# A four-layer graph network in fp32 on one core: whole-array transposes, a tanh kept in PSUM, one copy of s2 and an eleventh tile buffer

## The chip, the cores and the metric

The kernel runs on one core of a Trainium2 chip. The metric is the device time of that core in microseconds (us), as the median of several runs. All data are fp32.

## The reference

The input `x` has 64 graphs of 256 nodes with 128 features, and one weighted adjacency matrix `adj` (256 x 256) serves them all. Four layers follow each other; each takes `h = relu(layernorm(x))` and adds its result to `x`.

```
layer 0:  s1, s2 = h W1^T, h W2^T          (W from adj, 256 outputs e)
          e_ij = sum_e a_e leaky(s1_ie + s2_je + b_e) + adj_ij      (slope 0.2)
          x += sigmoid(softmax_j(e) h)
layer 1:  x_h = elu(h Wi + bi)
          e_ij = sigmoid(tgt_i + src_j + be) * mask_ij
          recv = elu([e x_h, x_h * sum_j e] Wn + bn);  x += [recv, x_h] Wm + bm
layer 2:  A = adj * exp(8 tanh((h q)(h k)^T / sqrt(128) / 8)), rows divided by their sums
          x += A h v
layer 3:  five steps of a gated unit: m = adj h; z, r = sigmoids, candidate = tanh; then x += h
```

The bulk of the work is `leaky(s1_ie + s2_je + b_e)` for all pairs of nodes: 64 graphs x 256 x 256 pairs x 256 values of e.

## The kernel before

**Layer 0's pairs.** A tile is one node i against all 256 nodes j of its graph, with 128 of the 256 values of e on the partitions: 128 x 256 elements. Eight tiles (four groups g, two halves ic) make a batch, which lies in one buffer `r` of the pool `rp` with `BUFS` = 10 buffers. Tiles are made by three engines: ACT with a Relu and a bias (line 620), POOL with a min and a max (line 625), DVE four tiles at a time from a copy `s2_dve` of `s2` in PSUM (line 608, half a batch). PE then multiplies a batch by `a_win` (line 673, `multiply`), four matmuls of N = 512, one for each group of 32 PSUM partitions, into the bank `e_ps`. Each fp32 matmul stands in the profile as two records of 128*32 (128 rows, 32 columns of the array), so a batch has eight records. A graph has 32 rows t and two values of ec for each, 64 batches. Where five complete batches (`SPARE`) wait for PE, `begin` makes the next row a merged one: the tiles of ec = 0 are made, and DVE adds those of ec = 1 into the same buffer (`merge`, line 642, eight instructions), so that PE has one batch to multiply in place of two. A merge thus moves work from PE to DVE.

**The rest of the layers** runs beside this, as Python generators that yield the engine which comes next: `head` and `senders` prepare layer 0's operands for the coming graphs, `softmax0` ends layer 0 of a graph, `layer1`, `layer2` and `layer3` follow for a group of two graphs (four blocks of 128 nodes; the first two and last two groups are of one graph). Each `Chain` runs its generators one after another at a pace in ns for each step: 2200 for layers 1 and 2 (`chain12`), 2400 for layer 3, 2500 for `softmax0`.

**The order of instructions** on all engines is fixed when the program is built. A planner (`Model`, and the loop at the end of the kernel) keeps a time for each engine, adds a cost in ns for every instruction, and always emits what can start first. `dve`, `act`, `pool`, `mm` hold these costs, `LAG` is the time from one engine to the next, and `MARGIN` gives paced steps of PE another 300. At run time each engine takes its instructions in that order and waits on semaphores.

**Matmuls and transposes.** `mm` splits every matmul into four, one for each group of 32 columns of the array:

```
        model.op("pe", max(n, 64) * 1.676)
        for c in range(4):
            nc.tensor.matmul(
                out[bass.ts(c, 32), :], lhsT=lhsT[:, bass.ts(c, 32)], rhs=rhs, **flags
            )
```

`tr` transposes a 128 x 128 block as such a matmul with the identity `ident` on the moving side. It serves `transpose_blocks` (tiles h0t, h_t, h3t), `softmax0` (`pm` into `e_ps`, which it reuses as `pt_ps`) and `layer3` (`hn_ps` after each of four steps, `y_ps` at the end).

**Layer 1's scores.** `tgt_ps`, one matmul for the group, lies in the single bank of `ps_a`; ACT writes `th = tanh(...)` for each graph to SBUF (line 793), and DVE makes `e_t` of it and of the mask `mask_h` (line 801). All of layers 1 and 2 take their PSUM from that one bank.

Of the kernel before, what the change touches and what calls it, by code (L numbers as in the profile page):

```python
# [16 lines left out]
FLT_MAX = 3.4028234663852886e38  # L17
STEPS = 5
INV_SQRT_D = 1.0 / (128.0 ** 0.5)
BUFS = 10  # L20
SPARE = 5
MARGIN = {"pe": 300}
MEMORY = 7000
# [30 lines left out]
def kernel(ctx: ExitStack, tc: tile.TileContext, ins: dict, out: bass.AP):  # L54
# [21 lines left out]
    def psum_a(shape, name):  # L76
        return ps_a.tile(shape, F32, tag="ps_a", name=name)
# [30 lines left out]
            )  # L108

    def tr(out, src):  # L110
        mm(out, lhsT=src, rhs=ident, start=True, stop=True)


    firsts = [sum(GROUPS[:g]) for g in range(len(GROUPS))]
# [328 lines left out]
    def transpose_blocks(space, src, tag, banks):  # L443

        yield "pe"
        G, _, W = sizes(src)
        tp = banks([P, G, P], tag + "_ps")
        for g in range(G):
            tr(tp[:, g, :], src[:, g, :])
        yield "act"  # L450
        t = space.tile([P, G, P], F32, tag=tag, name=tag)
        act(W).copy(t, tp)
        return t
# [77 lines left out]
    class Pairs:  # L531
# [36 lines left out]
        def own(self, who):  # L568

            if who == "dve" and who not in self.owned:  # L570
                t = self.owned[who] = ps_d.tile([P, 2, N], F32, tag="s2_dve", name="s2_dve")
                for ec in range(2):
                    dve(N).tensor_copy(t[:, ec, :], self.snd["s2"][:, ec, :])
            if who == "act":

                self.by_act += 1
                if self.by_act == 2:
                    t = self.owned[who] = ps_c.tile([P, 2, N], F32, tag="s2_act", name="s2_act")
                    act(2 * N, sbuf=1).copy(t, self.snd["s2"])
                if self.by_act <= 2:  # L580
                    return self.snd["s2"]
            return self.owned[who]
# [96 lines left out]
    def softmax0(g, b, of, e_ps, snd):  # L679


        h, xt = of["h"], xts[g]
        for ic in range(2):
            yield "dve", lambda: "adj_l" in snd

            if ic == 0:
                nmax = sp.tile([P, 2], F32, tag="nmax", name="nmax")
            dve(N, more=10).tensor_tensor_reduce(  # L688
                e_ps[:, ic, :], e_ps[:, ic, :], snd["adj_l"][:, ic, :], -1.0, FLT_MAX,
                ALU.add, ALU.min, nmax[:, ic : ic + 1],  # L690
            )
        for ic in range(2):
            yield "act"
            if ic == 0:
                pm = ap.tile([P, 2, N], F32, tag="pm", name="pm")
                rs = sp.tile([P, 2], F32, tag="rs", name="rs")
            act(N, 1, more=114).activation(  # L697
                pm[:, ic, :], e_ps[:, ic, :], AF.Exp, bias=nmax[:, ic : ic + 1], scale=-1.0,
                accum_out=rs[:, ic : ic + 1],
            )  # L700
        yield "dve"
        rh = sp.tile([P, 2], F32, tag="rh", name="rh")
        dve(2).reciprocal(rh, rs)
        yield "pe"
        pt_ps = e_ps
        for jc in range(2):
            for ic in range(2):
                tr(
                    pt_ps[:, jc, bass.ts(ic, P)], pm[:, ic, bass.ts(jc, P)]
                )  # L710
        yield "act"
        pt = ap.tile([P, 2, N], F32, tag="pt", name="pt")
        act(2 * N).activation(pt, pt_ps, AF.Copy, scale=0.5)
        yield "pe"
        o_ps = e_ps[:, :, 0:P]
        for ic in range(2):
            for jc in range(2):
                mm(
                    o_ps[:, ic, :], lhsT=pt[:, jc, bass.ts(ic, P)], rhs=h[:, b * 2 + jc, :],
                    start=(jc == 0), stop=(jc == 1),  # L720
                )
        for ic in range(2):
            yield "act"


            act(P, 2).activation(o_ps[:, ic, :], o_ps[:, ic, :], AF.Tanh, scale=rh[:, ic : ic + 1])
        yield "dve", lambda: counts["x1"] >= g - 2
        if b == 0:
            x1s[g] = ap.tile([P, 2 * GROUPS[g], P], F32, tag="x1", name="x1", bufs=3)
        x1 = x1s[g]  # L730
        dve(N).scalar_tensor_tensor(
            x1[:, bass.ts(b, 2), :], o_ps, 0.5, xt[:, bass.ts(b, 2), :], ALU.mult, ALU.add
        )
        if b == GROUPS[g] - 1:
            chain12.add(first_rest(g, x1))
# [16 lines left out]
    def layer1(x1):  # L752
# [8 lines left out]
        for b in range(NB):  # L761
# [13 lines left out]
            dve(2, 1).tensor_scalar(  # L775
                a_src[:, bass.ts(b, 2)], y_ps[:, :, P], 0.5, be_h, ALU.mult, ALU.add
            )
        yield "pe"
        tgt_ps = psum_a([P, W], "tgt_ps")
        mm(tgt_ps, lhsT=wt_rep, rhs=xh_t, start=True, stop=True)  # L780
        yield "pool"
        x1b = bp.tile([P, G, P], F32, tag="x1b", name="x1b")
        counts["x1"] += 1
# [1 line left out]
            x1b, x1, bm_bc.unsqueeze(1).to_broadcast([P, G, P]), ALU.add  # L785
        )

        ths, e_ts = [], []
        for b in range(NB):
            yield "act"  # L790
            th = bp.tile([P, 2, N], F32, tag="th", name="th", bufs=2)
            for jc in range(2):
                act(N, 1).activation(
                    th[:, jc, :], tgt_ps[:, bass.ts(b, N)], AF.Tanh,
                    bias=a_src[:, 2 * b + jc : 2 * b + jc + 1], scale=0.5,
                )
            ths.append(th)
        for b in range(NB):
            yield "dve"
            e_t = bp.tile([P, 2, N], F32, tag="e_t", name="e_t", bufs=2)  # L800
            dve(2 * N, more=200).scalar_tensor_tensor(e_t, ths[b], 1.0, mask_h, ALU.add, ALU.mult)
            e_ts.append(e_t)
        yield "pe"
        rsum_ps = psum_a([P, W], "rsum_ps")
# [106 lines left out]
    def layer3(x3, hn, h_t, home):  # L911
        G, NB, W = sizes(x3)
        hf = flat(h_t)
        for step in range(STEPS):
            yield "pe"
            m_ps = home.bank([P, W], "m_ps", step)
            for b in range(NB):
                for mc in range(2):
                    mm(
                        m_ps[:, bass.ts(b, N)], lhsT=hn[:, b * 2 + mc, :], rhs=adj_t[:, mc, :],  # L920
                        start=(mc == 0), stop=(mc == 1),
                    )
            g_ps = home.bank([P, W], "gate_ps", step + 1)
            mm(g_ps, lhsT=u3_t, rhs=hf, start=True, stop=False)
            yield "act"
            m_t = home.tile(W, "m_t", "m_t")
            act(W).copy(m_t, m_ps)  # L927
            yield "pe"
            mm(g_ps, lhsT=ws["w4_w"], rhs=m_t, start=False, stop=True)
            yield "act"  # L930

            t_r = m_ps
            act(W, 1).activation(t_r, g_ps, AF.Tanh, bias=br, scale=0.5)  # L933
            yield "dve"
            rh2 = home.tile(W, "rh2", "rh2")
            dve(W).scalar_tensor_tensor(rh2, t_r, 1.0, hf, ALU.add, ALU.mult)
            yield "pe"
            mm(
                g_ps, lhsT=w34_t, rhs=m_t, start=False, stop=True, skip_group_check=True
            )  # L940
            hv_ps = home.bank([P, W], "hv3_ps", step)
            mm(hv_ps, lhsT=ws["w5_w"], rhs=m_t, start=True, stop=False)
            mm(hv_ps, lhsT=u5_th, rhs=rh2, start=False, stop=True)
            yield "act"
            t_z, cand = g_ps, hv_ps
            act(W, 1).activation(t_z, g_ps, AF.Tanh, bias=bz, scale=0.5)  # L946
            yield "act"
            act(W, 1).activation(cand, hv_ps, AF.Tanh, bias=bh)  # L948

            yield "dve"  # L950
            df = home.tile(W, "rh2", "df")
            dve(W).tensor_tensor(df, cand, hf, ALU.subtract)
            yield "dve"
            zd = t_z
            dve(W).scalar_tensor_tensor(zd, t_z, 1.0, df, ALU.add, ALU.mult)
            yield "dve"
            hf_new = home.tile(W, "hf", "hf", 2)
            dve(W).scalar_tensor_tensor(hf_new, zd, 0.5, hf, ALU.mult, ALU.add)  # L958
            hf = hf_new
            counts["h3"] += step == 0  # L960
            if step < STEPS - 1:
                yield "pe"
                tp = home.bank([P, W], "hn_ps", step)
                for g in range(G):
                    tr(tp[:, bass.ts(g, P)], hf[:, bass.ts(g, P)])
                yield "act"
                hn = home.tile(W, "hn", "hn")
                act(W).copy(hn, tp)  # L968
                hn = hn.rearrange("p (g n) -> p g n", g=G)
        yield "pe"  # L970
        tp = home.bank([P, W], "y_ps", step)
        for g in range(G):
            tr(tp[:, bass.ts(g, P)], hf[:, bass.ts(g, P)])
        yield "dve"
        y = home.tile(W, "hn", "y").rearrange("p (g n) -> p g n", g=G)
        dve(W).tensor_tensor(y, tp.rearrange("p (g n) -> p g n", g=G), x3, ALU.add)
        return y
# [195 lines left out]
```

## Time and profile before

| What | Value |
|---|---|
| median of 3 runs | 5151.03 us (5151.01 to 5160.24) |
| the profiled execution | 5146.78 us |
| its span in the trace | 5144.3 us |
| granted TensorE clock | 0.998 |
| busy: PE, DVE, ACT, POOL | 98%, 97%, 98%, 95% |
| matmul records | 66800, of them 27632 of line 673 |
| DMA | 29.32 MB, mean 6 GB/s |

The profile is of one execution. "Busy" is the time in which at least one record of the engine is open. Records of PE, ACT and DVE overlap, because an instruction's record opens while the one before it still runs; so a mean duration is not the time that an instruction takes away from its engine, which is read from start to start in the timeline. A row of the costliest groups gives line, engine, operation, output and inputs, shapes and count, then busy us and mean ns of one, then the engine's idle time before them and what ended it. The windows give busy us and counts of PE, PE's weight loads, DVE, ACT and POOL in turn, then the granted clock, DMA's share and GB/s.

### The profile page before, as it was taken

The page shows a single profiled execution, that of the slowest core. Times are in us where ns is not written, and L with a number is a line of the kernel's source. Part 1 is how long each engine was busy: PE and PEld are TensorE (multiplying, and loading weights), DVE is VectorE, ACT ScalarE, POOL GpSimd, SP SyncE. Part 2 cuts the span into 40 slices and gives each one's busy share as a digit, 9 for nine tenths or more (in the row PEclk, how much of TensorE's full clock was granted, in tenths as well). Part 3 has the DMA queues.
Part 4 walks back from the last instruction along what each step waited for, and adds up shares of the span by engine and source line. Part 5 has one row for each costly group of instructions (what it writes and reads, how often), then busy time and mean ns, then how long its engine had stood idle before and what let it go on. Part 6 is the DMA issues. An engine that isn't in the chain of part 4 may idle for free. (4 is left out here: it accounts for less than half of the span.)

```text
span 5144.3 us, 172484 instructions
## 1 busy us (share of the span) xinstructions
PE 5063.0 (98%) x66800; PEld 2358.0 (46%) x66800; DVE 4983.5 (97%) x9900; ACT 5032.0 (98%) x13224; POOL 4895.6 (95%) x10829
## 2 busy tenths in 40 slices
PE   8999999999999999999999999999999999999997
PEld 4545444436444444544444544544444444444443
DVE  7999999999999999999999999999999999999994
ACT  7999999999999999999999999999999999999994
POOL 8999999999999999999999999999999999999992
PEclk9999999999999999999999999999999999999999
DMA  0000000000000000000000000000000000000000
GB/s 21 6 2 5 5 6 6 6 2 6 6 6 6 2 6 6 6 6 2 6 6 6 6 6 2 6 6 6 6 2 6 6 6 5 2 5 4 4 6 6
DMA packets 56104, 29.32 MB, mean 6 GB/s; under 512 B 20337, under 2 KB 55281, under 8 KB 55281
## 3 DMA queue, kind: packets, MB, share of 16 engines
q1 hardware_dynamic: 53168, 17.97, 1.4%
q8 instruction: 522, 8.55, 0.7%
q14 instruction: 302, 2.47, 0.2%
q10 hardware_dynamic: 2112, 0.33, 0.0%
HBM read 9.84 MB, written 8.45 MB: 4 GB/s over the span
## 5 line engine op out<-in xcount | busy, mean ns | idle before, releaser
L625 POOL TENSOR_SCALAR r<-s,s1n 128x256 f32<-128x256 f32 x10204 | 4646.4, 478 | 102.0 <-PE e_ps L673 33.5
L620 ACT ACTIVATE r<-s_act,s 128x256 f32<-128x256 f32 x9976 | 4593.6, 1478 | 10.5 <-PE e_ps L673 10.4
L673 PE MATMUL e_ps<-r,a_win 128*32 128x512 f32 x27632 | 3379.5, 593 | 9.8 <-POOL r L625 3.4
L642 DVE SCALAR_TENSOR_TENSOR r<-s_dve,s1n,r 128x256 f32<-128x256 f32 x5136 | 2093.8, 471 | 2.0 <-ACT r L620 1.0
L608 DVE TENSOR_TENSOR r<-s_dve,s1n 128x1024 f32<-128x1024 f32 x1735 | 2017.3, 1210 | 7.3 <-PE e_ps L673 1.4
L673 PEld LDWEIGHTS e_ps<-r,a_win 128*32 128x32 f32 x27632 | 1095.3, 110 | 1593.2 <-issue 1124.2
L620 ACT ACTIVATE r<-s,s 128x256 f32<-128x256 f32 x512 | 381.1, 1666 | 0.0
L437 ACT ACTIVATE h<-x,bsh,brs 128x128 f32<-128x128 f32 x384 | 329.8, 1386 | 3.6 <-POOL bsh L431 2.3
L946 ACT ACTIVATE gate_ps<-gate_ps,bz 128x512 f32<-128x512 f32 (+1 forms) x170 | 269.7, 1586 | 5.9 <-PE gate_ps L106 5.9
L948 ACT ACTIVATE hv_ps<-hv_ps,bh 128x512 f32<-128x512 f32 (+1 forms) x170 | 266.4, 1567 | 5.4 <-PE hv_ps L106 5.4
L106 PE MATMUL m_ps<-adj_t,hn 128*32 128x256 f32 x4096 | 268.1, 380 | 2.8 <-ACT hn L968 2.7
L927 ACT COPY m_t<-m_ps 128x512 f32<-128x512 f32 (+1 forms) x170 | 260.9, 1535 | 8.5 <-PE m_ps L106 8.5
L933 ACT ACTIVATE m_ps<-gate_ps,br 128x512 f32<-128x512 f32 (+1 forms) x170 | 256.9, 1511 | 9.2 <-PE gate_ps L106 8.8
L968 ACT COPY hn<-hn_ps 128x512 f32<-128x512 f32 (+1 forms) x136 | 208.1, 1530 | 20.6 <-PE hn_ps L106 20.5
L106 PEld LDWEIGHTS m_ps<-adj_t,hn 128*32 128x32 f32 x4096 | 157.5, 110 | 112.3 <-issue 31.9
L697 ACT ACTIVATE pm<-e_ps,nmax 128x256 f32<-128x256 f32 x128 | 195.0, 1531 | 2.2 <-DVE nmax L688 2.2
L106 PE MATMUL gate_ps<-m_t,t_w_w 128*32 128x512 f32 (+1 forms) x1360 | 187.3, 572 | 8.6 <-ACT m_t L927 7.8
L106 PE MATMUL gate_ps<-m_t,w_t 128*32 128x512 f32 (+1 forms) x1360 | 185.2, 568 | 3.1 <-ACT m_ps L933 3.1
L106 PE MATMUL hv_ps<-m_t,t_w_w 128*32 128x512 f32 (+1 forms) x1360 | 185.0, 567 | 0.0
L106 PE MATMUL hv_ps<-rh,u_th 128*32 128x512 f32 (+1 forms) x1360 | 184.9, 567 | 0.0
L106 PE MATMUL hn_ps<-ident,hf 128*32 128x128 f32 x4096 | 162.9, 274 | 12.5 <-DVE hf L958 12.5
L106 PEld LDWEIGHTS hn_ps<-ident,hf 128*32 128x32 f32 x4096 | 136.4, 110 | 77.0 <-issue 51.3
(206 smaller groups left out, 5951.7 us busy)
## 6 DMA issues: line engine op xcount, KB each, us to landing
xt<-in_x_dram SPq DMA_DIRECT2D x30, 256.0 KB
out_dram<-y SPq DMA_DIRECT2D x30, 256.0 KB
row<-rows SPq DMA_DIRECT2D x128, 0.5 KB
xt<-in_x_dram SPq DMA_DIRECT2D x4, 128.0 KB
out_dram<-y SPq DMA_DIRECT2D x4, 128.0 KB
bound<-row SPq DMA_DIRECT2D x30, 2.0 KB
raw_L_gnn_w_w<-in_L_gnn_w_w_dram SPq DMA_DIRECT2D x3, 128.0 KB
adj_n<-in_adj_dram ACTq DMA_DIRECT2D x1, 256.0 KB
```

Of the source, the lines that this page charges most:

```text
L106: nc.tensor.matmul(out[bass.ts(c, 32), :], lhsT=lhsT[:, bass.ts(c, 32)], rhs=rhs, **flags)
L437: act(P, 2, 1).activation(h[:, g, :], xt[:, g, :], AF.Relu, bias=shift[:, g : g + 1], scale=rstd[:, g : g + 1],)
L608: nc.vector.tensor_tensor(r[:, 2 * g2 : 2 * g2 + 2, :, :], s2[:, ec : ec + 1, :].unsqueeze(1).to_broadcast([P, 2, 2, N]), self.s1n_v[:, ec ...
L620: nc.scalar.activation(r[:, g, ic, :], s2[:, ec, :], AF.Relu, bias=s1[:, ec, i : i + 1])
L625: nc.gpsimd.tensor_scalar(r[:, g, ic, :], s2[:, ec, :], FLT_MAX, s1n[:, ec, i : i + 1], ALU.min, ALU.max,)
L642: nc.vector.scalar_tensor_tensor(r[:, g, ic, :], self.own("dve")[:, 1, :], self.of["s1n"][:, 1, i : i + 1], r[:, g, ic, :], ALU.max, ALU.add,)
L673: nc.tensor.matmul(self.e_ps[bass.ts(g, 32), :, :].rearrange("p a b -> p (a b)"), lhsT=a_win[:, batch["ec"], 31 - t : 63 - t], rhs=flat(r[ ...
L927: act(W).copy(m_t, m_ps)
L933: act(W, 1).activation(t_r, g_ps, AF.Tanh, bias=br, scale=0.5)
L946: act(W, 1).activation(t_z, g_ps, AF.Tanh, bias=bz, scale=0.5)
L948: act(W, 1).activation(cand, hv_ps, AF.Tanh, bias=bh)
L968: act(W).copy(hn, tp)
```

## The change

- `tr` no longer uses `mm`: it issues one `nc.tensor.transpose` on the whole 128 x 128 array. The planner counts 109 ns for it, and each group of transposes is preceded by `turn()`, which issues nothing and counts 245 ns of PE.
- `s2_dve` is copied by one instruction of 512 elements in place of two of 256, with 130 ns more in the planner.
- Layer 1 has one matmul for each graph into a bank `th_ps` (N = 256, two for a group, in place of one of 512). ACT writes both tanh blocks into that same bank, the second block first, since the first overwrites its own argument. DVE makes `e_t` from PSUM, and the planner no longer adds 200 ns to it. The steps go graph by graph: PE, ACT, DVE, PE, ACT, DVE.
- `BUFS` is 11. `pm` and `pt` of `softmax0` have one buffer each in place of two, and the two buffers of `th` are gone but for the small weights that are loaded into them at the start.

```diff
-BUFS = 10
+BUFS = 11
...
     def tr(out, src):
-        mm(out, lhsT=src, rhs=ident, start=True, stop=True)
+
+        model.op("pe", 109)
+        nc.tensor.transpose(out, src, ident)
+
+    def turn():
+
+        model.op("pe", 245)
...
         tp = banks([P, G, P], tag + "_ps")
+        turn()
         for g in range(G):
             tr(tp[:, g, :], src[:, g, :])
...
-                for ec in range(2):
-                    dve(N).tensor_copy(t[:, ec, :], self.snd["s2"][:, ec, :])
+                dve(2 * N, more=130).tensor_copy(t, self.snd["s2"])
...
-                pm = ap.tile([P, 2, N], F32, tag="pm", name="pm")
+                pm = ap.tile([P, 2, N], F32, tag="pm", name="pm", bufs=1)
...
         pt_ps = e_ps
+        turn()
...
-        pt = ap.tile([P, 2, N], F32, tag="pt", name="pt")
+        pt = ap.tile([P, 2, N], F32, tag="pt", name="pt", bufs=1)
...
-        yield "pe"
-        tgt_ps = psum_a([P, W], "tgt_ps")
-        mm(tgt_ps, lhsT=wt_rep, rhs=xh_t, start=True, stop=True)
...
-        ths, e_ts = [], []
+
+        e_ts = []
         for b in range(NB):
+            yield "pe"
+            th_ps = psum_a([P, 2, N], "th_ps")
+            mm(th_ps[:, 0, :], lhsT=wt_rep, rhs=xh_t[:, bass.ts(b, N)], start=True, stop=True)
             yield "act"
-            th = bp.tile([P, 2, N], F32, tag="th", name="th", bufs=2)
-            for jc in range(2):
+            for jc in (1, 0):
                 act(N, 1).activation(
-                    th[:, jc, :], tgt_ps[:, bass.ts(b, N)], AF.Tanh,
+                    th_ps[:, jc, :], th_ps[:, 0, :], AF.Tanh,
                     bias=a_src[:, 2 * b + jc : 2 * b + jc + 1], scale=0.5,
                 )
-            ths.append(th)
-        for b in range(NB):
             yield "dve"
             e_t = bp.tile([P, 2, N], F32, tag="e_t", name="e_t", bufs=2)
-            dve(2 * N, more=200).scalar_tensor_tensor(e_t, ths[b], 1.0, mask_h, ALU.add, ALU.mult)
+            dve(2 * N).scalar_tensor_tensor(e_t, th_ps, 1.0, mask_h, ALU.add, ALU.mult)
             e_ts.append(e_t)
```

`turn()` also stands ahead of the transposes into `hn_ps` and `y_ps` in `layer3`.

More of the change, by code (lines that the diff above doesn't have):

```diff
@@ L963, in layer3 @@
                 tp = home.bank([P, W], "hn_ps", step)
+                turn()
                 for g in range(G):
@@ L971, in layer3 @@
         tp = home.bank([P, W], "y_ps", step)
+        turn()
         for g in range(G):
```

## The prediction

> **What bounds the kernel now.** I read the engines' busy shares first, then the costliest groups, then the timeline of a steady stretch, the windows and the waits.
>
> ```profile
> PE 5063.0 (98%) x66800; PEld 2358.0 (46%) x66800; DVE 4983.5 (97%) x9900; ACT 5032.0 (98%) x13224; POOL 4895.6 (95%) x10829
> ...
> L625 POOL TENSOR_SCALAR r<-s,s1n 128x256 f32<-128x256 f32 x10204 | 4646.4, 478 | 102.0 <-PE e_ps L673 33.5
> ...
> L673 PE MATMUL e_ps<-r,a_win 128*32 128x512 f32 x27632 | 3379.5, 593 | 9.8 <-POOL r L625 3.4
> L642 DVE SCALAR_TENSOR_TENSOR r<-s_dve,s1n,r 128x256 f32<-128x256 f32 x5136 | 2093.8, 471 | 2.0 <-ACT r L620 1.0
> L608 DVE TENSOR_TENSOR r<-s_dve,s1n 128x1024 f32<-128x1024 f32 x1735 | 2017.3, 1210 | 7.3 <-PE e_ps L673 1.4
> ```
>
> Four engines are full at once, so no chain of waits sets the end, but shared capacity: layer 0's tiles `r` are made by POOL, ACT and DVE, PE multiplies them, and the planner merges two batches on DVE (L642) when PE lags. These records overlap, so I take costs from start to start in the timeline.
>
> ```profile
> 2559.69 6.62 PE L673 MATMUL e_ps<-r,a_win 128*32 128x512 f32 x60
> 2566.13 0.62 PE L106 MATMUL y_ps<-wn,xh_t 128*32 128x129 f32 x16
> ...
> 2567.42 1.08 PE L106 MATMUL hn_ps<-ident,hf 128*32 128x128 f32 x32
> 2568.30 4.50 PE L673 MATMUL e_ps<-r,a_win 128*32 128x512 f32 x40
> ```
> ```profile
> 2559.60 16.73 POOL L625 TENSOR_SCALAR r<-s,s1n 128x256 f32<-128x256 f32 x37
> 2576.29 1.28 POOL L784 TENSOR_TENSOR x1b<-x,bm_bc 128x512 f32<-128x512 f32 x1
> ```
> ```profile
> 2561.36 7.73 ACT L620 ACTIVATE r<-s_act,s 128x256 f32<-128x256 f32 x17
> 2567.42 1.93 ACT L773 COPY y<-y_ps 128x256 f32<-128x256 f32 x1
> ```
>
> PE: 60 records in 6.44 us, 107.3 ns each, 0.858 us per batch of eight; 32 records, which are four transposes, take 0.87 us (0.218 each). POOL: 16.69/37 = 0.451 us a tile. ACT: 6.06/17 = 0.357. DVE's timeline gives 5.76 us for five L608, rounded with the planner's 1.131 to 0.283 a tile, and 0.39 a merge. In such slots PE's records (35,072 of N=512, 11,776 of 256, 19,840 of 128 or 129) come to 4,941 us, 96% of the span: PE really is full. The windows say where this ends:
>
> ```profile
> 512.00:1024.00 512.00, 510.53 (x6772) 223.65 (x6768) 503.54 (x972) 510.92 (x1348) 498.42 (x1097) 1.00 0.02 6
> ...
> 5056.00:5100.00 44.00, 30.80 (x596) 17.37 (x592) 15.43 (x37) 17.67 (x41) 4.24 (x13) 1.00 0.03 8
> ```
>
> Only the last 90 us are latency, at a full clock of 1.00 in between.
>
> **What the Trainium skill says.** "TensorEngine Tiling (Array Packing)", Key Properties: changing the tiling mode drains TensorE; its Restrictions say that column tiling excludes transpose mode for fp32, so every turn to the whole array is a drain in and out. The trace has only 128*32 tiles and shows neither. "TensorE: Matmul & The Clock Gate", Part 4: a transpose takes about 275 ns in a kernel, and does not count as PE activity; a group of 0.7 us is short beside the 3.4 us window that Part 1 gives, so I expect the clock to stay. Here the records of the old transposes also last 273 ns, in slots of 27.3 (0.87/32), so 275 is a latency and no slot. "VectorE: DVE Perf Modes", the errata section, makes a PSUM source 62 cycles dearer than an SBUF one. The trace disagrees:
>
> ```profile
> L955 DVE SCALAR_TENSOR_TENSOR gate_ps<-gate_ps,df 128x512 f32<-128x512 f32 x150 | 103.0, 687 | 0.1
> ...
> L573 DVE COPY s_dve<-s 128x256 f32<-128x256 f32 x128 | 54.5, 426 | 7.6 <-ACT s L514 3.9
> ...
> L801 DVE SCALAR_TENSOR_TENSOR e_t<-th,mask_h 128x512 f32<-128x512 f32 x64 | 51.4, 803 | 0.0
> ```
>
> The same operation with one input in PSUM (L955) takes 687 ns, with both in SBUF (L801) 803; the measurement decides.
>
> **The change, part by part.**
> *Transposes.* The groups with `ident` have 11,264 records, 1,408 transposes, today 1,408 × 0.218 = 307 us of PE. They form 370 groups (34 each of h0t, h3t and y, 68 h_t, 64 pm, 136 hn). The new price is in no row. Below: one pass at a quarter of the old slot, no turn: 0.055. Above: 0.275 each, unpipelined, plus the turn. I take the diff's planner costs, 0.109 each and 0.245 a turn, since the planner's other costs agree with the trace (batch 858, POOL 453, ACT 357): 153 + 91 = 244 us. PE saves 63 us.
> *s2 copy.* One copy of 512 for two of 256. From L642 to L955 256 more elements cost 216 ns, so a copy's fixed part is about 426 − 216 = 0.21; ×64 = 13 us of DVE less.
> *e_t from PSUM.* 64 × 116 ns = 7 us of DVE less.
> *tanh into PSUM.* Two tanh take as long as two `r` tiles. "ScalarE: Activation LUTs", Step-by-step, calls PSUM the lower-latency target; no row isolates it. Bounds ±0.05 us × 128 = ±6 us of ACT, ±1.5 us of span; I take zero. The split matmul streams the same columns. New is a wait: the second block's matmul takes PSUM's only ps_a bank after the first block's e_t has been read. Everything on PE is queued behind it, and ACT's tanh and e_t wait for it. The planner puts it 450 ns after e_t's planned end, which covers it; uncovered it is at most 0.3 us in 32 groups, 10 us of PE, 3 us of span. I take 1. One more step of 2.2 us fits: chain12 has some 65 in the 160 us of a group.
> *Eleven buffers.* Waits of a maker for PE to free a buffer (total us, times, longest), from the list of waits:
>
> ```profile
> POOL r L625 <- PE e_ps L673: 33.5, 25, 6.0
> ...
> ACT r L620 <- PE e_ps L673: 10.4, 10, 2.8
> ```
>
> With DVE's 1.4 that is 74 + 29 + 5 = 108 tiles. Between none and all; I take half, 54. *pm and pt single:* nothing, since a graph comes every 80 us and its softmax has some 11 steps of 2.5 us; if that cover went, ACT would wait for PE once a graph.
> In the tail a group of two transposes takes 0.46 us for 0.44: nothing. No DMA is moved and no queue's order depends on one.
>
> *The sum.* If the end comes T us sooner, the makers lose T × (1/0.451 + 1/0.357 + 1/0.283) = 8.55 T tiles. A batch that PE can take again (0.858 us) spares 8 merges, 3.14 us of DVE, which are 11.1 tiles, and asks for 8: a gain of 3.1, 3.59 tiles per us of PE. PE gets back 63 − T. So 12.14 T = 3.59 × 63 + 20/0.283 + 54 = 226 + 71 + 54, T = 29, less 1 for the new wait: **28 us**. The profiled execution took 5146.8 us with a span of 5144.3; it becomes 5119. The median of the runs is 4.3 us above it: **5123**.
>
> **The rivals.**
> *Slower: turns too dear.* One mechanism, PE's drain at the 370 turns. T = (125 + 3.59 × (154 − 0.370 x)) / 12.14 for a turn of x ns: nil at 510, a group of four at 0.95 us against 0.87 now. At 700 ns it is −20 us, 5171; at 0.275 a transpose −40, 5191. For it speaks that every group drains twice and loads fresh weights; against it, that PE's records show a latency of some 273 ns for N=128, so two drains would have to be wholly bare. 8%.
> *Two passes.* If the transpose still runs fp32 in two passes, it does not do what it says: 0.218 each plus the turn, PE loses 91 us, T = −17, 5168. 4%.
> *PE's time is not taken up.* The order is fixed by the planner; if PE's saved time turns into waiting for tiles, only DVE's 20 us count, 71/12.14 = 6 us: 5145. PE's 4% of empty slots speak for it, the merge rule against it. 9%.
> *Cheaper turns.* A turn beside idle time costs nothing, and all buffer waits go: T up to 60, 5091; in the middle 45, 5106. The lower bound of both prices together (PE saves 230 us, T = 83, 5068) I hold for unlikely. 13%.
> The forecast itself: 66%, 5108 to 5138, from the tanh bound, the wait and the buffers.
>
> **How the numbers follow.** 0.2%, 10 us, is about what a measurement of this kernel can tell from none. Faster: 66 + 13 and a point of the third case, 80%; same 9%; slower 11%. The range 5094 to 5147 takes in the forecast, most of the cheaper turns and of PE's unused time, and leaves out the two slower cases and the far end of the cheap one.
>
> **What would show it.** The ident groups fall to an eighth of their records or so (hn_ps 4096 to 512); from the first transpose of four to the next operation 0.6 to 0.75 us; merges (L642's x5136) fall by 8 × (63 − 28)/0.858, to about 4,810; the copy of s2 stands 64 times at about 640 ns; e_t near 690; POOL's wait for e_ps under 20 us. A group over 0.95 us, or merges that stay while PE has gaps, would make it wrong.

## The result, and the profile after

The changed kernel takes 5139.52 us (median of 6 runs, 5136.74 to 5146.74) and the kernel before, beside it, 5158.78 us: a ratio of 0.9966, interval 0.9956 to 0.9976. A second set of runs gave 0.9977 (0.9968 to 0.9985). So it is faster, by 12 to 19 us where 28 were forecast. In the first set the kernel before has two runs at 5,151 and four at 5,158 to 5,162 us, the changed kernel five at 5,137 to 5,141 and one at 5,147, so the 19 us come in part from how these groups are mixed; group against group, and in the second set, the gain is about 12 us.

The two profiled executions happen to take the same time (5146.78 and 5146.74 us, spans 5144.3 and 5144.9), since they come from different sets of runs: ACT's tile takes 364.5 ns from end to end in the first trace and 365.2 in the second, which on 13,200 ACT instructions is some 9 us (an estimate). I set counts, slots and idle times of the two traces against each other, and not their spans.

The engines and the costliest groups of the changed kernel, from its page:

```profile
PE 5058.0 (98%) x57347; PEld 1988.1 (39%) x57347; DVE 4951.3 (96%) x9664; ACT 5034.1 (98%) x13196; POOL 4862.2 (95%) x10825
...
L631 POOL TENSOR_SCALAR r<-s,s1n 128x256 f32<-128x256 f32 x10200 | 4612.8, 475 | 81.0 <-PE e_ps L679 21.9
L626 ACT ACTIVATE r<-s_act,s 128x256 f32<-128x256 f32 x9948 | 4489.0, 1312 | 2.6 <-PE e_ps L679 2.6
L679 PE MATMUL e_ps<-r,a_win 128*32 128x512 f32 x27872 | 3330.9, 594 | 5.6 <-POOL r L631 2.3
L614 DVE TENSOR_TENSOR r<-s_dve,s1n 128x1024 f32<-128x1024 f32 x1803 | 2093.9, 1211 | 4.7
L648 DVE SCALAR_TENSOR_TENSOR r<-s_dve,s1n,r 128x256 f32<-128x256 f32 x4896 | 2002.3, 472 | 1.0 <-POOL r L631 1.0
```

PE multiplies (27,872 − 27,632)/8 = 30 batches more, DVE merges 240 tiles fewer. DVE and POOL are less busy than before by 32 and 33 us; ACT is not. The steady stretch says it best; first the kernel before, then the changed one (length; busy PE, its weight loads, DVE, ACT, POOL; clock, DMA, GB/s):

```profile
160.00:4900.00 4740.00, 4705.42 (x61934) 2176.99 (x61930) 4680.23 (x9275) 4731.25 (x12447) 4620.88 (x10207) 1.00 0.02 5
```
```profile
160.00:4900.00 4740.00, 4696.97 (x53276) 1845.95 (x53278) 4650.18 (x9045) 4734.65 (x12424) 4593.00 (x10212) 1.00 0.02 5
```

ACT has 5 us left of 4,740, and had 9 before. DVE has 90 (60 before) and POOL 147 (119): what the change took from them turned into idle time. The granted clock stays at 1.00 here, as forecast.

The transposes, in PE's timeline of the changed kernel:

```profile
2582.76 1.90 PE L679 MATMUL e_ps<-r,a_win 128*32 128x512 f32 x16
2584.59 0.66 PE L113 MATMUL hn_ps<-ident,hf 128*128 128x128 f32 x4
2585.18 1.93 PE L679 MATMUL e_ps<-r,a_win 128*32 128x512 f32 x16
```

Sixteen records before the group need 16 × 0.1073 = 1.72 us, but the group starts 1.83 us after them: 0.11 us for the turn in. From its first transpose to the next operation are 0.59 us. A group thus takes 0.70 us, against 0.87 before and 0.68 in the forecast.

The other two parts, from DVE's groups of the changed kernel (busy, mean ns, idle before):

```profile
L579 DVE COPY s_dve<-s 128x512 f32<-128x512 f32 x64 | 44.1, 689 | 5.1 <-ACT s L521 3.9
L806 DVE SCALAR_TENSOR_TENSOR e_t<-th_ps,mask_h 128x512 f32<-128x512 f32 x64 | 43.8, 684 | 9.4 <-ACT th_ps L800 9.0
```

One copy is 689 ns for twice 426; about 640 were expected. From end to end the copy takes 729 ns where the pair took 924 (medians), 12 us in all for the forecast's 13. e_t takes 684 for 803, as expected; it now also waits for its tanh, 9 us in all.

### The profile page after: what moved, and what is told of

Read it like the earlier page. It is cut to its first block, busy times and chain, and to the rows that moved or that the text cites. A ratio compares the mean times of both kernels' runs of the same rounds, so it can differ in the third digit from the quotient of the medians.

```text
span 5144.9 us, 152945 instructions
## 1 busy us (share of the span) xinstructions
PE 5058.0 (98%) x57347; PEld 1988.1 (39%) x57347; DVE 4951.3 (96%) x9664; ACT 5034.1 (98%) x13196; POOL 4862.2 (95%) x10825
## 5 line engine op out<-in xcount | busy, mean ns | idle before, releaser
L631 POOL TENSOR_SCALAR r<-s,s1n 128x256 f32<-128x256 f32 x10200 | 4612.8, 475 | 81.0 <-PE e_ps L679 21.9
L626 ACT ACTIVATE r<-s_act,s 128x256 f32<-128x256 f32 x9948 | 4489.0, 1312 | 2.6 <-PE e_ps L679 2.6
L679 PE MATMUL e_ps<-r,a_win 128*32 128x512 f32 x27872 | 3330.9, 594 | 5.6 <-POOL r L631 2.3
L614 DVE TENSOR_TENSOR r<-s_dve,s1n 128x1024 f32<-128x1024 f32 x1803 | 2093.9, 1211 | 4.7
L648 DVE SCALAR_TENSOR_TENSOR r<-s_dve,s1n,r 128x256 f32<-128x256 f32 x4896 | 2002.3, 472 | 1.0 <-POOL r L631 1.0
L679 PEld LDWEIGHTS e_ps<-r,a_win 128*32 128x32 f32 x27872 | 958.1, 110 | 1734.4 <-issue 1255.6
L626 ACT ACTIVATE r<-s,s 128x256 f32<-128x256 f32 x512 | 311.1, 1207 | 0.0
L951 ACT ACTIVATE gate_ps<-gate_ps,bz 128x512 f32<-128x512 f32 (+1 forms) x170 | 236.6, 1392 | 7.0 <-PE gate_ps L106 6.9
L106 PE MATMUL s_ps<-h0t,w_p 128*32 128x256 f32 (+1 forms) x1568 | 139.4, 449 | 5.4 <-ACT s1n L482 2.8
L106 PE MATMUL gate_ps<-hf,u_t 128*32 128x512 f32 (+1 forms) x1088 | 143.9, 574 | 0.0
```

Source lines behind the costliest of these rows:

```text
L106: nc.tensor.matmul(out[bass.ts(c, 32), :], lhsT=lhsT[:, bass.ts(c, 32)], rhs=rhs, **flags)
L614: nc.vector.tensor_tensor(r[:, 2 * g2 : 2 * g2 + 2, :, :], s2[:, ec : ec + 1, :].unsqueeze(1).to_broadcast([P, 2, 2, N]), self.s1n_v[:, ec ...
L626: nc.scalar.activation(r[:, g, ic, :], s2[:, ec, :], AF.Relu, bias=s1[:, ec, i : i + 1])
L631: nc.gpsimd.tensor_scalar(r[:, g, ic, :], s2[:, ec, :], FLT_MAX, s1n[:, ec, i : i + 1], ALU.min, ALU.max,)
L648: nc.vector.scalar_tensor_tensor(r[:, g, ic, :], self.own("dve")[:, 1, :], self.of["s1n"][:, 1, i : i + 1], r[:, g, ic, :], ALU.max, ALU.add,)
L679: nc.tensor.matmul(self.e_ps[bass.ts(g, 32), :, :].rearrange("p a b -> p (a b)"), lhsT=a_win[:, batch["ec"], 31 - t : 63 - t], rhs=flat(r[ ...
```

## The experiments

Each kernel is one edit of the kernel before or of the changed one. Ratios are to the kernel before in the same set; the sets are e1 to e4, e5 to e8, e9 to e12, e13 to e16, and e17 with e18. Across sets a ratio tells less: e2 and e9 are one kernel and have 0.9848 and 0.9867, because the kernel before took 5158.5 us in one set and 5147.5 in the other.

**ACT's price.** In the timeline of the kernel before this line stands ahead of the 17 tiles of ACT that the prediction reads (start, length, ...):

```profile
2561.11 1.77 ACT L773 COPY y<-y_ps 128x256 f32<-128x256 f32 x1
```

From start to start the 17 tiles take 6.06 us, 0.357 each. But ACT's records open early and overlap: the costliest group has a mean record of 1,478 ns before, four times the distance from one tile to the next. The copy ahead ends at 2561.11 + 1.77 = 2562.88, and the last of the tiles, whose line is 2561.36 and 7.73 long, at 2569.09: from end to end 6.21 us, 0.365 each. Over all neighbouring tiles of the trace the median is 356 ns between starts and 364 between ends (357 and 365 in the changed kernel). The planner charges 357.

*e1, the changed kernel again.*

> The changed kernel as it stands, so that the other three kernels stand beside it on the same chip. Three theories of why the gain was under 28 us. A: ACT alone is full (7 us idle between 160 and 5000 us in the trace after, where DVE has 91 and POOL 153): the planner charges ACT 357 ns for a tile r, which is the distance from start to start, while the ends of successive tiles lie 365 to 366 ns apart; with some 13,200 ACT instructions each some 9 ns too cheap, ACT is handed about 115 us more than its share, and time given back to PE and DVE turns into idle time. B: PE's turns to the whole array are dearer than planned, so PE never got its 63 us. C: the new order of layer 1's scores costs it: the second tanh waits for the first (482 ns for 339 in the trace after), and e_t for both. Here all three expect what was measured: 0.9966 of before, within 0.001.

Measured: 5146.5 us, before 5158.53, ratio 0.9977 (0.9968 to 0.9985).

*e2, ACT's costs raised in the changed kernel; e3, the same in the kernel before.*

```diff
-    TILE = {"act": 357, "pool": 453}
+    TILE = {"act": 366, "pool": 453}
...
-        model.op("act", 40 + n * 0.833 + 42 * sbuf + (0, 103, 196)[pointers] + 49 * table + more)
+        model.op("act", 48.5 + n * 0.833 + 42 * sbuf + (0, 103, 196)[pointers] + 49 * table + more)
```

> The changed kernel with only the planner's costs for ACT raised: 366 for a tile r (357 before), and 8.5 ns more for every other ACT instruction; nothing else is touched, so the planner hands some tiles of ACT to POOL and DVE. A: 40 to 80 us shorter than the changed kernel (0.984 to 0.992 of it), since ACT's 115 us too much are shared out over four engines; PE, DVE and POOL lose idle time. B and C: within 10 us of the changed kernel, since no turn and no wait goes away.

Measured: 5079.71 us, 0.9848 (0.9835 to 0.9862); 67 us less than e1 beside it.

> The kernel before with the same two costs raised and no part of the change. A: also 40 to 80 us shorter than before, and with ACT priced rightly in both the change is worth what was forecast, about 25 to 28 us (the second of these kernels 0.5% below this one). B: no gain from the costs, and the change stays worth 17 us or less in this pair as well. C: the same as B.

Measured: 5120.85 us, 0.9927 (0.9915 to 0.9939); 38 us less than before, just under the 40 to 80 that A expected. The pair e3 to e2 differs by 41 us, more than the 28 forecast and the 25 to 28 that A expected. The same stretch in e2 and in e3:

```profile
160.00:4900.00 4740.00, 4732.61 (x54319) 1854.55 (x54315) 4721.93 (x9079) 4723.75 (x12346) 4684.87 (x10417) 1.00 0.02 5
```
```profile
160.00:4900.00 4740.00, 4726.19 (x62517) 2456.12 (x62514) 4719.79 (x9210) 4686.76 (x12256) 4679.86 (x10333) 1.00 0.02 5
```

In e2 ACT and DVE are about equally full and POOL's idle time falls from 147 to 55 us; ACT makes 10,220 tiles for 10,460, some 88 us of its time. In e3 ACT now waits 53 us. No turn and no wait was taken away; only some nine nanoseconds in a table were changed. So it is shown that ACT's price held the changed kernel back, as theory A says, and B doesn't explain it. No other price was tried, so 366 need not be the best.

**The parts alone.**

*e4, the transposes alone in the kernel before.*

```diff
-        mm(out, lhsT=src, rhs=ident, start=True, stop=True)
+        model.op("pe", 109)
+        nc.tensor.transpose(out, src, ident)
```

(with `turn()` ahead of each group)

> The kernel before with the whole-array transposes alone (and the planner's 109 and 245 ns for them). Forecast for this part: 226/12.14 = 19 us. A: less, since only ACT's share of it shortens the end: 8 to 15 us. B: no gain, or slower than before. C: the whole gain and more, 17 to 22 us, because the part that costs is left out.

Measured: 5137.34 us, 0.9959 (0.9947 to 0.9972), 21 us. This part alone gains 9 us more than the whole change, e1, beside it. B is out. The size lies above A's 8 to 15 and within C's 17 to 22; but ACT has 40 tiles less than in the kernel before (10,448 for 10,488), which are 15 us by themselves. Against e1 the last tile is made 3 us earlier (5031.3 for 5034.6 us after the start), and the tail, from the last tile to the end, is 5 us shorter (105.1 for 110.2): the order of instructions has a part in it. (The bulk, below, is all up to the last tile.)

*e5, the tanh in PSUM alone* (the hunks of `layer1`).

> The kernel before with the tanh in PSUM alone (ten buffers, old transposes, two copies of s2). In this program ACT has 10,456 tiles, 32 fewer than before. A (ACT sets the end): 32 x 0.366 = 12 us less of ACT, and 64 pairs of tanh that take 0.82 us for 0.73, 6 us more: 4 to 9 us shorter than before. B: 0 to 3 us shorter, since PE gains nothing here. C (this part costs): slower than before, by 3 to 9 us.

Measured: 5147.73 us, 1.0001 (0.9993 to 1.0009). Neither A's gain nor C's loss. Its trace, of an execution of 5154.38 us, names parts that make about nothing together: ACT has 32 tiles less, 12 us, but the tanh pairs cost 6 us more, ACT's idle time grew by 3, and the tail is 108.0 us for 103.8.

*e6, ten buffers.*

```diff
-BUFS = 11
+BUFS = 10
```

> The changed kernel with ten buffers in place of eleven, nothing else. In this program ACT has 10,424 tiles, 36 fewer than with eleven, and DVE 4,696 merges, 200 fewer. A: 36 x 0.366 = 13 us less of ACT, so 8 to 15 us shorter than the changed kernel. B: unchanged within 3 us. Forecast, where the eleventh buffer spares makers waits worth half of 108 tiles: 4 to 5 us longer than the changed kernel.

Measured: 5130.72 us, 0.997 (0.9958 to 0.9981). The changed kernel wasn't run in this set, so its 0.9966 and 0.9977 tell little here. The traces tell more: those of e6, of e7 and of e1 all have ACT's tile at 365.2 ns from end to end. The spans of e1, e6 and e7, from their pages:

```profile
span 5144.8 us, 152945 instructions
```
```profile
span 5136.9 us, 153539 instructions
```
```profile
span 5130.6 us, 152915 instructions
```

e6 is 8 us shorter than e1, the last tile 6.7 us earlier (5027.9 for 5034.6), as A has it with 36 tiles of ACT fewer. The forecast's loss isn't there: by these traces the eleventh buffer costs time in this plan.

*e7, a step between the two tanh.*

```diff
-            yield "act"
             for jc in (1, 0):
+                yield "act"
                 act(N, 1).activation(
```

> The changed kernel with a step between the two tanh of a graph, so that other ACT work may stand between them; the second no longer waits bare for the first to leave the shared bank. ACT has 10,460 tiles as in the changed kernel. A: 64 x 0.088 = 5.6 us less of ACT, so 4 to 7 us shorter than the changed kernel. C: the same 6 us and also the 9 us for which DVE waits before e_t, up to 15 us. B: nothing.

Measured: 5125.61 us, 0.996 (0.9948 to 0.9973). Trace against trace it is 14 us shorter than e1: the last tile is made 5.7 us earlier (5028.9), as A has it, and the tail is 8.5 us shorter (101.7 for 110.2), which together comes near C's 15. Between 160 and 4,900 us ACT has 2.7 us of idle time, the least of all. That one kernel gains so much in its tail need not be the step's doing (see e14).

*e8, the one copy alone.*

```diff
-                for ec in range(2):
-                    dve(N).tensor_copy(t[:, ec, :], self.snd["s2"][:, ec, :])
+                dve(2 * N, more=130).tensor_copy(t, self.snd["s2"])
```

> The kernel before with the one copy of s2 alone. ACT has 10,484 tiles, 4 fewer than before; the copy takes 0.73 us for 0.95, 14 us of DVE less. A: DVE's time is idle time already, and ACT's falls by 1.5 us: 0 to 3 us shorter. Forecast: 71 tiles of DVE less in a shared capacity, 3 to 4 us (the two can't be told apart by this run alone). C: the same as the forecast.

Measured: 5144.69 us, 0.9994 (0.9985 to 1.0002). About nothing.

**The parts once ACT is priced rightly**, beside e9, e2's kernel in this set.

> The changed kernel with ACT's planner costs raised, again, so that the next three stand beside it on the same chip. All theories: 0.985 of before, as measured.

Measured: 5079.33 us, 0.9867 (0.9853 to 0.9882).

*e10, e9 with e7's step.*

> The same with a step between the two tanh of a graph. ACT has 10,208 tiles, 12 fewer. If ACT still sets the end: 5.6 us of waiting and 4 us of tiles less, 8 to 12 us shorter than without the step. If the four engines now share the work: 5.6 us x 0.2265 = 1.3 us and a little for e_t's wait, 1 to 4 us shorter.

Measured: 5085.95 us, 0.988 (0.9865 to 0.9895): 7 us longer by the medians (5082.6 to 5089.4 us), which nobody expected. In the trace the last tile is made at the same time (4973.4 us after the start for 4973.6), so the bulk gained nothing; the tail is 113.7 us for 103.9, in another order of the last layers.

*e11, e9 with ten buffers.*

> The changed kernel with ACT's planner costs raised and ten buffers. ACT has 10,200 tiles, 20 fewer, and DVE 4,640 merges, 56 fewer. If ACT still sets the end: 7 us shorter than with eleven. If the engines share: within 3 us. Forecast's step (the eleventh buffer spares waits): 4 to 5 us longer.

Measured: 5085.81 us, 0.988 (0.9864 to 0.9897), 6 us longer, near the forecast's step of 4 to 5; but it is the sum of a bulk that is 18 us longer and a tail that is 12 us shorter.

*e12, e9 with the old transposes.*

```diff
-        model.op("pe", 109)
-        nc.tensor.transpose(out, src, ident)
+        mm(out, lhsT=src, rhs=ident, start=True, stop=True)
```

(and no cost for `turn`)

> The changed kernel with ACT's planner costs raised and the old transposes in four column tiles, priced as before. ACT has 10,264 tiles, 44 more. Forecast's step for the transposes in a shared capacity: 226/12.14 = 19 us longer than with the whole-array transposes. If ACT still set the end: 44 x 0.366 = 16 us longer. If the turns give nothing once ACT is priced rightly: within 5 us.

Measured: 5093.07 us, 0.9894 (0.9879 to 0.9908): the transposes are worth 14 us there, three quarters of the forecast.

**What the order alone does, and POOL.**

*e13, e3 with the one copy; e14, the changed kernel with another margin; e15, e2 with it; e16, e3 with the transposes.*

```diff
-MARGIN = {"pe": 300}
+MARGIN = {"pe": 310}
```

> The kernel before with ACT's planner costs raised and the one copy of s2. With ACT priced rightly DVE is the fullest engine of that kernel (20 us idle between 160 and 5000 us, ACT 56), and its two copies are priced 666 ns together where their slots take 946. If DVE sets the end there: 64 x 0.21 = 14 us of DVE less and a plan that fits, 10 to 18 us shorter than without the copy. Forecast's step in a shared capacity: 4 us shorter.

Measured: 5142.84 us, 0.997 (0.9959 to 0.9982).

> The changed kernel with PE's margin in the planner 310 ns for 300, which means nothing by itself and only puts instructions in another order. If differences of some 5 to 10 us between these kernels come from the order that falls out (the tail, and where waits fall): up to 10 us from the changed kernel, either way. If the parts alone decide: within 3 us.

Measured: 5144.81 us, 0.9974 (0.9964 to 0.9984); e1 had 5146.5, with the kernel before at 5158.5 both times. The sum changes little, but not its parts: the last tile is made 10 us later than in e1 (5044.6 for 5034.6), and the tail is 11 us shorter (98.9 for 110.2). So the order alone moves either part by some 10 us, and no single step of that size in the other experiments can be credited to its edit without doubt.

> The changed kernel with ACT's planner costs raised and PE's margin 310 for 300. The same two readings: up to 10 us from 5079.5 us if the order matters, within 3 us if not.

Measured: 5097.33 us, 0.9882 (0.9869 to 0.9896), 18 us over e2 and e9, where either reading allowed 10 at most.

> The kernel before with ACT's planner costs raised and the whole-array transposes alone. Forecast's step: 19 us shorter than without them. If DVE sets the end there: the planner takes merges from DVE, so again most of it, 10 to 19 us. If the transposes don't pay: within 3 us.

Measured: 5128.23 us, 0.9945 (0.9932 to 0.9959), against 5120.85 of e3.

Taken across sets, all three kernels with ACT priced rightly came out 7 to 22 us longer than their partners. Two causes offered themselves. The first was a wait: ACT waits for POOL's shift `bsh` ahead of a layer's normalisation, here in e2 and then in e15 (total us, times, longest), and 56.7 us in e13 for 32.1 in e3, in both cases longer by about the missing time.

```profile
ACT h L443 <- POOL bsh L437: 13.9, 9, 10.1
```
```profile
ACT h L443 <- POOL bsh L437: 31.6, 60, 10.1
```

*e17, e13 with more margin for ACT; e18, e15 with it.*

```diff
-MARGIN = {"pe": 300}
+MARGIN = {"pe": 300, "act": 600}
```

(e18 has 310 and 600 in place of 310 alone)

> The kernel before with ACT's planner costs raised, the one copy, and in the planner 600 ns of margin for paced steps of ACT where they had 100, so that ACT comes to a layer's normalisation later than POOL has its shift bsh. In the kernel without this margin ACT's wait for bsh comes to 56.7 us in 83 waits (13.9 us in 9 in the fastest kernel, most of it at the start). If that wait made it 22 us slower than its partner without the copy: the wait falls under 25 us and the time to 5100 to 5125 us. If it is only a sign of an order that is slow for another reason: 5135 us or more.

Measured: 5135.86 us, 0.9962 (0.9949 to 0.9974); the wait fell to 31.3 us.

> The changed kernel with ACT's planner costs raised and PE's margin 310 (5097 us, 31.6 us of ACT's wait for bsh in 60 waits), and the same 600 ns of margin for ACT. If the wait made the 18 us over 5079 us: it falls under 18 us and the time to 5076 to 5086 us. If not: 5093 us or more.

Measured: 5094.48 us, 0.9879 (0.9863 to 0.9894); the wait fell to 21.9 us.

The wait fell by 25 and 10 us and the time by 7 and 3, of which the kernel before, 2 us shorter in this set, may account for 2: the wait is a sign, not the cause. The second candidate is POOL itself. Its row in e2, then in e15 (minimum, median and maximum ns):

```profile
L631 POOL TENSOR_SCALAR r<-s,s1n x10280: 463/475/1025, 23.9 to 4972.2; 128x256 f32<-128x256 f32 x198
```
```profile
L631 POOL TENSOR_SCALAR r<-s,s1n x10276: 466/477/902, 24.0 to 4990.4; 128x256 f32<-128x256 f32 x198
```

Every tile takes two to three ns more in e15, with the same instruction. From end to end of neighbouring tiles the mean is 451.6 ns in e2 and e9, 453.9 in e15 and e18; times 10,114 tiles that is 23 us, and POOL has only some 50 us of idle time left there. e13, e16 and e17 show the same shift against e3. It goes with the set and not with the kernel: e14 has it against the changed kernel as well, where POOL has time to spare. That it makes the missing 18 us is likely and not shown, since the order of e15 is another too. So I compare kernels in which POOL is nearly full only within a set, and what e13, e15 and e16 were to tell stays open. Within their set the changed kernel with ACT priced rightly (e15) is 31 us below e16 and 46 below e13, which has the direction and about the size of the 41 between e3 and e2, though e16 and e13 already hold a part of the change. Why POOL's slot differs between sets isn't shown.

## Why the prediction was right and wrong

**The step that failed is "Four engines are full at once", and with it the exchange "12.14 T".** ACT alone was full: 9 us of 4,740 were idle before, where PE had 35, DVE 60 and POOL 119, and the windows of the kernel before could have told. In the changed kernel ACT had 5 and the others 43 to 147. A shared capacity that ends 28 us sooner takes 28/0.357 = 78 tiles from ACT; the plan took 28.

The term beneath it is "ACT: 6.06/17 = 0.357". I read it from starts, as the rule stated ahead of the prediction has it, and took the planner's equal figure as a confirmation; from end to end the slot is 0.364 to 0.365. In the sum itself this hardly counts, but the planner divides the work by 357. On the 9,948 tiles that read PSUM ACT is handed some 80 us more than planned (an estimate from 365.2 − 357); the shortfall of its other instructions, to which e2 adds 8.5 ns each, wasn't measured by itself. e2 shows the cause in one edit: the same change with ACT repriced takes 67 us less. The chance given to "PE's time is not taken up", 9%, was too small; what happened is its mechanism in part. That e4's 21 us lie near the forecast's 19 for the transposes is luck, since the 19 come from the exchange that did not hold.

**Transposes: right.** 0.70 us for a group of four against 0.68 forecast, and hn_ps stands 512 times. By these medians PE got back about 56 us of the forecast's 63: 0.17 us for each of 334 groups of four, and a little less than nothing for the 36 of two. Of this, 30 batches, 26 us, were used; 41 batches had been forecast. "TensorEngine Tiling (Array Packing)", Key Properties, has the drain, and the trace agrees: 0.11 us lie ahead of the group, and the four starts are 165, 109 and 109 ns apart, with 202 to the next operation. So the turn costs about 0.26 us, and the rival of dear turns is out. e12 prices the part at 14 us for 19 where ACT doesn't set the end.

**Copy and e_t on DVE: right in size, and worth nothing here that can be told**, since DVE's time is idle time: e8 0.9994, e5 1.0001 (with its tanh). That `pm` and `pt` with one buffer each cost nothing wasn't tried alone.

**A term left out: POOL.** "e_t from PSUM" was costed on DVE alone. In the kernel before POOL stands still while DVE makes e_t from two SBUF inputs; its timeline beside the two e_t that DVE has at 2583.60 and 2586.93 us:

```profile
2582.97 5.09 POOL L625 TENSOR_SCALAR r<-s,s1n 128x256 f32<-128x256 f32 x9
```

Nine tiles at 0.451 need 4.06 us; they take 5.09. In the changed kernel a stretch that holds an e_t too (at 2578.61):

```profile
2573.69 8.59 POOL L631 TENSOR_SCALAR r<-s,s1n 128x256 f32<-128x256 f32 x19
```

0.452 each, with no stall. In the trace before 63 of POOL's tiles after 100 us take over 600 ns, and each overlaps one of the e_t; together they lose 31 us. In every kernel with th_ps there is none, from the end of one tile to the end of the next (in e5 to e7 many records are that long, but not these distances). "SBUF — State Buffer", Who interferes with whom, says that a DVE instruction with two SBUF inputs contends with a GpSimd instruction that reads SBUF; the trace agrees, and I should have used it. The prediction's 803 ns for e_t is a mean; the median is 732, and the shortest is 674 ns in both kernels, so the gap to PSUM may be this meeting seen from DVE (not tried apart). In the change as it stands POOL's 31 us are idle time; from e3 to e2 POOL's tiles take 39 us less, 32 of them such stalls, which may be why the pair's 41 us exceed the 28.

**The wait at th_ps** was placed on PE; it fell on ACT and DVE. ACT's timeline in the changed kernel:

```profile
2581.27 1.91 ACT L626 ACTIVATE r<-s_act,s 128x256 f32<-128x256 f32 x5
2583.05 0.94 ACT L800 ACTIVATE th_ps<-th_ps,a_src 128x256 f32<-128x256 f32 x2
```

From the end of the tiles (2583.18) to that of the pair (2583.99) are 0.81 us, for 0.73 before. The second tanh overwrites what the first reads: from end to end the two take 339 and 482 ns, for 365 each before. That is 0.09 us a pair, 6 us of the one engine that had none to give. In e7, where other ACT work may stand between, all have a median of 339, and its last tile is 5.7 us earlier: the delay is the second's wait for the first. With ACT repriced the step gained nothing (e10).

**Eleven buffers.** The waits for a free buffer, after:

```profile
POOL r L631 <- PE e_ps L679: 21.9, 18, 4.5
...
ACT r L626 <- PE e_ps L679: 2.6, 2, 1.3
```

They were 33.5 and 10.4 us: nearly half of them went, as forecast, though POOL's 21.9 stayed above the 20 named. They were POOL's for the most part, where time was idle; and the plan with eleven buffers gave ACT 36 tiles more, so that ten are about 8 us faster by the traces (e6). With ACT repriced ten were 6 us slower (e11).

**The tail** was costed at nothing. The stretch whose line before is in the prediction:

```profile
5056.00:5100.00 44.00, 34.67 (x460) 15.66 (x456) 14.44 (x34) 16.60 (x36) 2.51 (x9) 0.89 0.02 7
```

It is all latency again, with the clock down to 0.89 for 1.00. From the last tile to the end it is 103.8 us before and 110.2 after, and 91.7 to 113.7 in the experiments. In both kernels layer 3's last five steps, from their first m_t to the end, take the same 47 us; the difference lies in the layers ahead of them, in whatever order they come. The clock doesn't decide it: in the 60 us after the last tile e8 has 0.94 and a tail of 95.7 us, e6 0.97 and one of 109.0. Nor are the whole-array transposes needed for a lower clock there: e13, with the old ones, has 0.91. These differences are as large as the smaller parts of the change, and no step of mine could have foretold it.

## What to carry to other kernels

Where an engine's records overlap, take its slot from end to end over a long run of one instruction, and check it against the engine's idle time: an engine with no gaps, while the others have some, is the bound, whatever its planned cost. In this order, fixed by a cost table, an engine priced too cheap by two per cent became the only bound, and work saved on the others turned into idle time; correcting the table was worth 67 us in the changed kernel and 38 in the one before, where the change was worth 12 to 19 (e2, 5080 us, is the fastest kernel here with its second run, e9). Where small edits put all instructions in another order, look at the bulk and the tail apart. Ask of every VectorE instruction with two SBUF inputs what it does to GpSimd beside it.

## What was not expected of the hardware

- ACT's 128x256 tile: 356 ns between starts, 364 between ends (median before); between two ACT instructions that are not tiles it is the other way about (means 438 and 385 before), so the difference is absorbed there.
- The same distance between ends is 364.4 to 364.5 ns in the traces before, e8 and e9 to e12, and 365.1 to 365.2 in the others, 0.2%; e2 and e9, one kernel, lie on either side with the same time, while the kernel before took 11 us less in e9's set. What decides it isn't shown.
- A tanh that overwrites in place the bank that another has just read ends 482 ns after it, against 339 for the first of the pair, and 365 for each with SBUF as target.
- POOL's tile of the same shape took 451.6 ns in one set of runs and 453.9 in another, 0.5%, and nothing in the kernels accounts for it.
- One e_t with both inputs in SBUF held POOL's tile beside it for some 490 ns (31 us over 63; one of the 64 did not).
